# Two key stages in hand-written order on VectorE and ScalarE, layer 0 one stage later, x put away in between

## The chip, the cores and the metric

The kernel runs on one core of one Trainium2 chip. The metric is the device time of one execution in microseconds (us). Before the change it is 2494.17 us, the median of three runs (2492.08 to 2495.93).

## What is computed

The reference is a small decoder with two layers on two sequences (batch 2) of 512 tokens of width 1024, with a context of 1024 rows per sequence. All matrix products that matter here are in float32, except the first.

```python
x = x + L0_xattn(layernorm(x), ctx)      # both fake-quantized to 0..255, then x1 @ ctx
x = x + L0_ffn(layernorm(x))             # linear layer, plus a LoRA that a router weights
x = x + L1_xattn(layernorm(x), ctx)      # 32 query heads, 8 key/value heads of 128, rope on q and k
x = x + L1_ffn(layernorm(x))             # linear layer, plus the LoRA of one of 4 experts
```

The part that the change touches is the start: the product of layer 0 (the first line) and the keys and values of layer 1, which need the context alone and so can be made before x is ready:

```python
k = (ctx @ wk); k = k * cos + rotate_half(k) * sin      # 1024 x 1024 by 1024 x 1024, per sequence
v = (ctx @ wv)
q1, q2 = clip(round(x1 / s1 + z1), 0, 255), clip(round(ctx / s2 + z2), 0, 255)
layer0 = ((q1 - z1) * s1) @ ((q2 - z2) * s2)
```

## The kernel before

**Products.** Each large product is cut into two by two quarters and done with seven products instead of eight. The sums of quarters that this needs are made on VectorE: four for a weight (`left_steps`, lines 242 to 254) and four for the context (`right_steps`, lines 256 to 268). Products 1 and 2 need the raw quarters alone, so they can start before the sums. `seven` (line 270) takes the products in the order 1, 2, 6, 7, 5, 4, 3. Products 1 and 2, 7 and 4, 5 and 3 add into the same PSUM bank; there are four banks under the tag "b". So product 4 may begin only when VectorE has read 7 (line 291), and product 3 only when it has read 5 (line 293). After products 2, 5, 4 and 3 a result is complete. For keys it gets its rope (`rope_steps`, line 213: two half copies on ScalarE, lines 216 and 217, then lines 219, 222 and 223 on VectorE, in place for three of the four results) and goes to DRAM from SyncE's queue (line 476). Values go there without rope (line 500).

**Stages.** There are four stages per sequence: keys of weight half 0 and 1, values of weight half 0 and 1. Each has two groups of seven products. For sequence 0 the first two products of all four key groups are written first (lines 1015 to 1030); then the loop at line 1034 runs the rest stage by stage.

**Layer 0.** `quantized_product(b)` (line 396) is a Python generator that runs beside the stages: `weave` (line 335) calls it once after every second product. One sequence takes 14 calls: four that load and quantize two blocks of 128 context rows each (lines 194, 197 and 198 on VectorE), four that take the layernorm of 128 rows of x (lines 163 to 176), quantize them and sum each row (lines 420 to 422), where the third and fourth also transpose the block two behind (`turned`), one that transposes the third block, one for the last and the column sums, and four products of bfloat16 numbers. Calls go on through both sequences. x is loaded at the head of the generator and stays in SBUF until layer 0's linear layer, which comes after the keys and values.

**Buffers.** Tiles come from tags with a fixed number of buffers: u8 (14 of 8 KB per partition: context quarters and their sums, x, quantized rows), u4 (17 of 4 KB: weight quarters and their sums, context rows, layernorm results), u2 (10), small (16).

**Order.** Every instruction is written for one engine[...]. TensorE's order is the written one (line 976). VectorE's is the written one only within lines 1015 to 1030 for the instructions written there; others that are ready may come between. All else, the DMA queues of SyncE and ScalarE too, is ordered by a planner, which works through the program with estimated times and takes what is ready, the earlier written first.

The lines in question, as they stand before:

```python
    w[1][:] = quad_sums(wk_raw[1])
    side = chain(quantized_product(0), quantized_product(1))
    ...
            if b == 0 and i < 2:
                main = chain(*first[i])
    ...
            weave(main, side, 2, 8 if b == 0 and i == 0 else 0)
```

Of the kernel before, what the change touches and what calls it, by code (L numbers as in the profile page):

```python
# [14 lines left out]
AF = mybir.ActivationFunctionType  # L15
ALU = mybir.AluOpType
# [23 lines left out]
def decoder_kernel(  # L40
# [339 lines left out]
    q_d = [[spill([P, S], f"q{b}_{hd}") for hd in range(NH)] for b in range(B)]  # L380
    wo_d = [{i: spill([P, 2, HALF], f"wo{g}_{i}") for i in (4, 5, 6, 7)} for g in range(NKV)]


    def context_quarter(b, ch, kh, queue):
        t = u8([P, 4, HALF])
# [10 lines left out]
    def quantized_product(b):  # L396
        x[b] = halves()
        for t in range(NT):
            nc.sync.dma_start(rows(b, t), x_in[b, ts(t, P), :])
        q2 = [u8([P, 4, D], BF16) for _ in range(2)]  # L400
        for k in range(NKT):
            c_t = u4([P, D])
            nc.sync.dma_start(c_t, ctx_in[b, ts(k, P), :])
            quantized(q2[k // 4][:, k % 4, :], c_t, "x2")
            if k % 2:
                yield
        x1T = u8([P, NC, S], BF16)
        rsum, l1s = [], []

        def turned(t):  # L410
            tr = ps_wide().bitcast(BF16)[:, 0 : NC * P].rearrange("p (c n) -> p c n", c=NC)
            for c in range(NC):
                nc.tensor.transpose(tr[:, c, :], l1s[t][:, ts(c, P)], ident_b)
            copy_out(x1T[:, :, ts(t, P)], tr)

        for t in range(NT):
            h = layernorm(rows(b, t))
            l1 = u2([P, D], BF16)
            quantized(l1, h, "x1")
            r = small([P, 1])  # L420
            nc.scalar.activation(h, l1, AF.Copy, accum_out=r)
            nc.vector.tensor_scalar(r, r, c_x2, None, ALU.mult)
            rsum.append(r)
            l1s.append(l1)
            if t > 1:
                turned(t - 2)
            yield
        turned(NT - 2)
        yield
        turned(NT - 1)  # L430


        cs = ps_wide()
        for n in range(2):
            for k in range(NKT):
                nc.tensor.matmul(
                    cs[:, ts(n, HALF)],
                    ones_b,
                    q2[k // 4][:, k % 4, ts(n, HALF)],
                    start=(k == 0),  # L440
                    stop=(k == NKT - 1),
                )
        csum = u4([P, D])
        nc.vector.tensor_scalar(csum, cs, kc2, c_x1, ALU.add, ALU.mult)
        yield
        for t in range(NT):
            acc = ps_wide()
# [12 lines left out]
            nc.vector.scalar_tensor_tensor(xs, y, s12, xs, ALU.mult, ALU.add)  # L460
            yield
# [374 lines left out]
    def attention(extra):  # L836

        total = B * NH
        heads, outs, kv = {}, {}, {}
        stretches = iter(())

        def begin(n):
            if n >= total:
                return
            gg = n // GRP
            if gg not in kv:
                b, g = gg // NKV, gg % NKV  # L850
                kT = u4([P, S2])
                nc.sync.dma_start(kT, kT_d[b][g])
                v = u4([P, NKT, DH])
                nc.sync.dma_start(v, v_d[b][g // 2][:, :, ts(g % 2, DH)])
                kv[gg] = kT, v
                outs[gg] = u8([P, GRP, S])
            heads[n] = Head(n, kv[gg], outs[gg][:, n % GRP, :])

        begin(0)
        for n in range(-2, total + GRP + 1):  # L860
            new, mid, old = heads.get(n + 2), heads.get(n + 1), heads.get(n)
            begin(n + 3)
            if new:
                for j in range(4):
                    new.scores(j)
            yield

            if n - 1 in heads:
                heads.pop(n - 1).normalize()
            if n == GRP - 1 or n == NH:  # L870
                x[n // NH] = halves()
                for t, d in zip(x[n // NH], x_d[n // NH]):
                    nc.sync.dma_start(t, d)

            if GRP <= n <= total and n % GRP == 0:
                oT = outs.pop(n // GRP - 1)
                sums = u8([P, 3, 2, 256])
                places = iter(range(3))
                o_ops = left_sums(
                    nc.gpsimd,  # L880
                    oT[:, 0:2, 0:256],
                    oT[:, 2:4, 0:256],
                    oT[:, 0:2, 256:S],
                    oT[:, 2:4, 256:S],
                    lambda: sums[:, next(places)],
                )
# [12 lines left out]
            for _ in range(extra.pop(n, 0)):  # L899
                next(extra["products"])  # L900
                next(tree, None)
            if n == GRP:
                w_ops = {i: output_operand(0, i) for i in (1, 6, 2, 7, 5, 4, 3)}
            for steps in (tree, *extra["later"]):
                for _ in steps:
                    pass
            extra["later"].clear()
            yield

            if mid:  # L910
                mid.place_maximum()
            if old:
                old.turn_sum()
                old.attend(0)
            if mid:
                mid.exponential(0)
            if old:
                old.den = from_row(old.den)
            if new:
                new.turn_maximum()  # L920
            if mid:
                mid.exponential(1)
            if new:
                new.nmx = from_row(new.nmx)
            if old:
                old.attend(1)
            yield
# [84 lines left out]
    ctx_ops = [ctx_raw[0], ctx_raw[2]] + [None] * 5  # L1012
    w = [wk_raw[q][0:2] + [None] * 5 for q in range(2)]
    first = [keys(0, q, ctx_ops, w[q]) for q in range(2)]
    with tc.manual_schedule(engines={mybir.EngineType.DVE}):
        rights = right_steps(nc.vector, *ctx_raw, lambda: u8([P, 4, HALF]))
        lefts = left_steps(nc.vector, *wk_raw[0], lambda: u4([P, 4, 256]))
        advance(rights, 2)
# [9 lines left out]
        for _ in range(2):  # L1028
            for g in first[1]:
                next(g)  # L1030
    w[1][:] = quad_sums(wk_raw[1])

    side = chain(quantized_product(0), quantized_product(1))
    for b in range(B):
        if b == 1:
            ctx_raw = [context_quarter(1, ch, kh, nc.scalar) for ch in range(2) for kh in range(2)]
            w = quad_weights(wk, 0)
            ctx_ops = context_sums(ctx_raw)
        for i, stage in enumerate((keys, keys, values, values)):
            if b == 0 and i < 2:  # L1040
                main = chain(*first[i])
            else:
                main = pair(*stage(b, i % 2, ctx_ops, w))
            weave(main, side, 2, 8 if b == 0 and i == 0 else 0)
            if i < 3 and (b, i) != (0, 0):
                w = quad_weights((wk, wv)[(i + 1) // 2], (i + 1) % 2)
            if i == 1 and b == 1:
                for _ in side:
# [3 lines left out]
                nc.sync.dma_start(a_t, a0T.rearrange("(c p) m -> p c m", p=P))  # L1052
                nc.gpsimd.dma_start(b_t, b0.partition_broadcast(P))  # L1053
                tT = [None] * B
                hs, steps = normed(0, u8, 2)
                side = chain(steps, routed(0, hs, a_t, b_t, tT))
    for _ in side:
# [17 lines left out]
    for b in range(B):  # L1075
# [6 lines left out]
        weave(main, side, 1 + b, 3)  # L1082
        for _ in side:
            pass

    def put_away(b):
        for t, d in zip(x[b], x_d[b]):
            nc.sync.dma_start(d, t)

    put_away(0)  # L1090
    w = [quad_weights(wq, 0), quad_weights(wq, 1)]
# [59 lines left out]
            wupT[ts(ch, 4 * P), ts(nh, HALF)].rearrange("(c p) n -> p c n", p=P),  # L1151
        )

    def fetch_rows():
        x[0] = halves()
        for t, d in zip(x[0], x_d[0]):
            nc.sync.dma_start(t, d)

    def begin_map():
        hs = last["hs"]  # L1160
        last["h"][:2] = hs[0]
# [5 lines left out]
    for i in range(2):  # L1167
# [5 lines left out]
    hooks[(61, 2)] = [  # L1173
        lambda: fetch_weight(1, 0, 0),
        lambda: fetch_weight(2, 1, 0),
        fetch_rows,
        begin_map,
    ]
    hooks[(62, 1)] = [lambda: advance(last["gates"], 4)]
# [136 lines left out]
```

## Time and profile before

| What | us |
|---|---|
| Median of three runs | 2494.17 |
| The profiled execution | 2491.89 |
| Its span, first to last instruction | 2490.1 |
| TensorE busy | 2434.2 |
| VectorE busy | 1852.5 |
| GpSimd busy | 1011.8 |
| ScalarE busy | 527.9 |

The span is what the trace covers; the execution's own time lies 1.8 us above it. TensorE is busy almost throughout, so what counts are the stretches in which it waits. Keys and values of both sequences, with layer 0, take about the first 420 us of the span; in that stretch TensorE is busy 398.2 us. A float32 product of 128 x 512 is seen in the trace as two matmul records. "L291" is line 291 of the kernel; a bracket in a timeline gives the idle time of the engine just before the instruction and what ended it.

### The profile page before, as it was taken

The page shows a single profiled execution, that of the slowest core. Times are in us where ns is not written, and L with a number is a line of the kernel's source. Part 1 is how long each engine was busy: PE and PEld are TensorE (multiplying, and loading weights), DVE is VectorE, ACT ScalarE, POOL GpSimd, SP SyncE. Part 2 cuts the span into 40 slices and gives each one's busy share as a digit, 9 for nine tenths or more (in the row PEclk, how much of TensorE's full clock was granted, in tenths as well). Part 3 has the DMA queues.
Part 4 walks back from the last instruction along what each step waited for, and adds up shares of the span by engine and source line. Part 5 has one row for each costly group of instructions (what it writes and reads, how often), then busy time and mean ns, then how long its engine had stood idle before and what let it go on. Part 6 is the DMA issues. An engine that isn't in the chain of part 4 may idle for free.

```text
span 2490.1 us, 19684 instructions
## 1 busy us (share of the span) xinstructions
PE 2434.2 (98%) x6848; PEld 1214.5 (49%) x6856; DVE 1852.5 (74%) x2036; ACT 527.9 (21%) x615; POOL 1011.8 (41%) x536
## 2 busy tenths in 40 slices
PE   7999999999999998989999999999999999999999
PEld 3477458654444443434444444444444444445454
DVE  5848774345886557988888888888898888887552
ACT  1201221011222222232222222222222222222100
POOL 0000010111000001557676767676777676667421
PEclk8999999999999999999999999999999999999999
DMA  7225233012895221343323322442334233323301
GB/s 264 103 92 204 75 124 106 26 68 106 283 329 199 76 93 47 102 131 107 84 80 109 109 83 80 138 150 79 114 106 130 62 104 114 104 74 110 127 26 43
DMA packets 148243, 283.83 MB, mean 114 GB/s; under 512 B 29296, under 2 KB 47232, under 8 KB 146352
## 3 DMA queue, kind: packets, MB, share of 16 engines
q1 hardware_dynamic: 107888, 242.25, 28.7%
q10 hardware_dynamic: 39824, 39.60, 6.6%
q8 instruction: 55, 0.90, 0.2%
q0 software_dynamic: 432, 0.71, 0.1%
q14 instruction: 44, 0.36, 0.0%
HBM read 221.44 MB, written 61.08 MB: 113 GB/s over the span
## 4 chain that ended last, share of the span: by engine, by line
PE 59%; DVE 7%; POOL 2%; issue 2%; DMA 1%; ACT 1%; SPq 0%; POOLq 0%; DVEq 0%; ACTq 0%
PE b L347 26%; PE wide L748 15%; PE b L811 15%; PE wide L712 2%; DVE u L794 2%; DMA u<-in_wo_dram 1%; PE wide L937 1%; DVE u L772 1%; DVE u L774 1%; DVE small L714 1%; POOL u L804 1%; POOL u L803 0%; DVE u L762 0%; DVE u L222 0%; DVE u L219 0%
## 5 line engine op out<-in xcount | busy, mean ns | idle before, releaser
L347 PE MATMUL b<-u,u 128*128 128x512 f32 (+1 forms) x3648 | 1408.6, 543 | 25.3 <-DVE u L291 10.8
L347 PEld LDWEIGHTS b<-u,u 128*128 128x128 f32 x3648 | 691.4, 191 | 707.5 <-issue 619.4
L748 PE MATMUL wide<-u,u 128*128 128x512 f32 x1024 | 456.9, 597 | 15.7 <-DVE small L714 8.5
L811 PE MATMUL b<-u,u 128*128 128x512 f32 x1024 | 461.2, 593 | 0.0
L800 POOL TENSOR_TENSOR u<-u 128x1024 f32<-128x1024 f32 x64 | 151.6, 2369 | 747.4 <-DMA row<-small 385.0
L762 DVE TENSOR_TENSOR u<-wide,u 128x1024 f32<-128x1024 f32 x256 | 312.7, 1224 | 128.2 <-PE wide L748 127.8
L797 ACT ACTIVATE u<-u 128x2048 f32<-128x2048 f32 x128 | 244.6, 1911 | 675.7 <-DVE u L794 626.4
L748 PEld LDWEIGHTS wide<-u,u 128*128 128x128 f32 x1024 | 193.4, 191 | 268.0 <-issue 176.8
L794 DVE TENSOR_TENSOR u<-u,b 128x2048 f32<-128x2048 f32 x128 | 290.0, 2266 | 0.0
L811 PEld LDWEIGHTS b<-u,u 128*128 128x128 f32 x1024 | 186.7, 192 | 185.2 <-issue 185.2
L322 POOL TENSOR_TENSOR u<-u,u 128x512 f32<-128x512 f32 x120 | 189.4, 1599 | 195.0 <-DVE u L320 175.4
L320 DVE TENSOR_TENSOR u<-u,b 128x512 f32<-128x512 f32 x200 | 135.7, 679 | 135.1 <-PE b L347 135.1
L803 POOL TENSOR_TENSOR u<-u,u 128x1024 f32<-128x1024 f32 x64 | 150.8, 2356 | 35.6 <-ACT u L797 34.6
L804 POOL TENSOR_TENSOR u<-u,u 128x1024 f32<-128x1024 f32 x64 | 151.9, 2374 | 5.0
L822 POOL TENSOR_TENSOR u<-u,u 128x512 f32<-128x512 f32 x64 | 119.9, 1873 | 21.4 <-DMA u<-row 21.4
L1053 POOL DMA_DIRECT2D u<-in_b_dram x1 | 0.6, 558 | 301.8 <-PE wide L450 301.8
L216 ACT ACTIVATE u<-u 64x512 f32<-64x512 f32 x72 | 45.2, 628 | 344.6 <-DVE u L293 167.3
L712 PEld LDWEIGHTS wide<-ident,u 128*128 128x128 f32 x512 | 80.2, 204 | 64.6 <-issue 54.7
L770 DVE TENSOR_TENSOR u<-u 128x1024 f32<-128x1024 f32 x64 | 111.4, 1741 | 0.0
L772 DVE TENSOR_TENSOR u<-u,u 128x1024 f32<-128x1024 f32 x64 | 106.3, 1660 | 0.2
L805 POOL TENSOR_TENSOR u<-u 128x512 f32<-128x512 f32 x64 | 102.0, 1594 | 5.0
L774 DVE TENSOR_TENSOR u<-u,u 128x1024 f32<-128x1024 f32 x64 | 97.4, 1522 | 0.2
(125 smaller groups left out, 1552.3 us busy)
## 6 DMA issues: line engine op xcount, KB each, us to landing
u<-row ACTq DMA_DIRECT2D x128, 256.0 KB, 3.7
u<-wo SPq DMA_DIRECT2D x64, 512.0 KB, 4.0
u<-in_wo_dram SPq DMA_DIRECT2D x48, 512.0 KB, 4.5
u<-in_wq_dram SPq DMA_DIRECT2D x32, 512.0 KB, 4.0
q<-u SPq DMA_DIRECT2D x64, 256.0 KB, 2.1
u<-in_wo_dram SPq DMA_DIRECT2D x16, 1024.0 KB, 8.1
wo<-u SPq DMA_DIRECT2D x32, 512.0 KB, 3.7
u<-q SPq DMA_DIRECT2D x64, 256.0 KB, 4.1
```

The lines of the kernel that those rows point to most:

```text
L320: nc.vector.tensor_tensor(c, c, acc, ALU.add)
L322: nc.gpsimd.tensor_tensor(c, c, u, ALU.add)
L347: nc.tensor.matmul(acc, lhsT, rhs, start=start and k == 0, stop=k == len(pairs) - 1, skip_group_check=True,)
L748: nc.tensor.matmul(sc[:, ts(n, HALF)], self.kT[:, ts(2 * j + n, P)], self.qT, start=True, stop=True,)
L762: nc.vector.tensor_tensor(self.e[j // 2][:, js, :], sc.rearrange("p (k q) -> p k q", k=2), mask[j], ALU.add)
L772: nc.vector.tensor_tensor(m, m, e[1][:, 0:2, :], ALU.max)
L794: nc.vector.tensor_tensor(e, e, self.nmf.unsqueeze(1).to_broadcast([P, 4, S]), ALU.add)
L797: nc.scalar.activation(e, e, AF.Exp)
L800: nc.gpsimd.tensor_tensor(d, e[:, 0:2, :], e[:, 2:4, :], ALU.add)
L803: nc.gpsimd.tensor_tensor(d, d, e[:, 0:2, :], ALU.add)
L804: nc.gpsimd.tensor_tensor(d, d, e[:, 2:4, :], ALU.add)
L811: nc.tensor.matmul(self.acc, self.v[:, k, :], self.e[j][:, k % 4, :], start=(k == 0), stop=(k == NKT - 1),)
```

## The change

It has five parts.

1. The first two key stages of sequence 0, whole, stand in a block in which VectorE and ScalarE keep the written order. The four sums of the second weight half are written after results 5 to 8 of the first stage (g0's last product and g1's first three). The sums of the first value weight (`wv`) are written at the end of this block.
2. Layer 0 begins in the second key stage instead of late in the first: five calls there, none before.
3. The row sums move from the block's own call into `turned`, so they stand two blocks behind. The row sum's ScalarE pass writes its unused copy to a new u4 tile instead of over the layernorm result.
4. Once layer 0 is done for sequence 0, its x goes to DRAM (`put_away(0)`), and it is fetched again (`fetch_rows(0)`) before the layernorm of the linear layer.
5. Two of the four context quarters of sequence 1, the ones that its first two products read, are loaded before the last value stage of sequence 0; the other two stay where they were.

`put_away` and `fetch_rows` existed before and are moved up; `fetch_rows` takes the sequence as an argument now.

```diff
@@ quantized_product, turned
             copy_out(x1T[:, :, ts(t, P)], tr)
+            r = small([P, 1])
+            nc.scalar.activation(u4([P, D]), l1s[t], AF.Copy, accum_out=r)
+            nc.vector.tensor_scalar(r, r, c_x2, None, ALU.mult)
+            rsum.append(r)
...
             quantized(l1, h, "x1")
-            r = small([P, 1])
-            nc.scalar.activation(h, l1, AF.Copy, accum_out=r)
-            nc.vector.tensor_scalar(r, r, c_x2, None, ALU.mult)
-            rsum.append(r)
             l1s.append(l1)
@@
-    with tc.manual_schedule(engines={mybir.EngineType.DVE}):
+
+    def layer_0():
+        yield from quantized_product(0)
+        put_away(0)
+        yield from quantized_product(1)
+
+    side = layer_0()
+    with tc.manual_schedule(engines={mybir.EngineType.DVE, mybir.EngineType.Activation}):
         rights = right_steps(nc.vector, *ctx_raw, lambda: u8([P, 4, HALF]))
...
         for _ in range(2):
             for g in first[1]:
                 next(g)
-    w[1][:] = quad_sums(wk_raw[1])
-
-    side = chain(quantized_product(0), quantized_product(1))
+        lefts = left_steps(nc.vector, *wk_raw[1], lambda: u4([P, 4, 256]))
+        for i, _ in enumerate(chain(*first[0])):
+            if i in (4, 5, 6, 7):
+                w[1][:] = next(lefts) or w[1]
+        weave(chain(*first[1]), side, 2)
+        w = quad_weights(wv, 0)
+
     for b in range(B):
         if b == 1:
-            ctx_raw = [context_quarter(1, ch, kh, nc.scalar) for ch in range(2) for kh in range(2)]
+            for ch in range(2):
+                ctx_raw[2 * ch + 1] = context_quarter(1, ch, 1, nc.scalar)
             w = quad_weights(wk, 0)
             ctx_ops = context_sums(ctx_raw)
         for i, stage in enumerate((keys, keys, values, values)):
             if b == 0 and i < 2:
-                main = chain(*first[i])
-            else:
-                main = pair(*stage(b, i % 2, ctx_ops, w))
-            weave(main, side, 2, 8 if b == 0 and i == 0 else 0)
-            if i < 3 and (b, i) != (0, 0):
+                continue
+            if (b, i) == (0, 3):
+                ctx_raw = [None] * 4
+                for ch in range(2):
+                    ctx_raw[2 * ch] = context_quarter(1, ch, 0, nc.scalar)
+            weave(pair(*stage(b, i % 2, ctx_ops, w)), side, 2)
+            if i < 3:
                 w = quad_weights((wk, wv)[(i + 1) // 2], (i + 1) % 2)
             if i == 1 and b == 1:
...
                 tT = [None] * B
+                fetch_rows(0)
                 hs, steps = normed(0, u8, 2)
```

More of the change, by code (lines that the diff above doesn't have):

```diff
@@ L381, in decoder_kernel, with put_away, fetch_rows @@
     wo_d = [{i: spill([P, 2, HALF], f"wo{g}_{i}") for i in (4, 5, 6, 7)} for g in range(NKV)]
+    def put_away(b):
+        for t, d in zip(x[b], x_d[b]):
+            nc.sync.dma_start(d, t)
+    def fetch_rows(b):
+        x[b] = halves()
+        for t, d in zip(x[b], x_d[b]):
+            nc.sync.dma_start(t, d)
     def context_quarter(b, ch, kh, queue):
@@ L870, in attention @@
             if n == GRP - 1 or n == NH:
-                x[n // NH] = halves()
-                for t, d in zip(x[n // NH], x_d[n // NH]):
-                    nc.sync.dma_start(t, d)
+                fetch_rows(n // NH)
             if GRP <= n <= total and n % GRP == 0:
@@ L1084, in decoder_kernel @@
             pass
-    def put_away(b):
-        for t, d in zip(x[b], x_d[b]):
-            nc.sync.dma_start(d, t)
     put_away(0)
@@ L1152, in fetch_weight @@
         )
[L1154 to L1157, printed above, removed]
     def begin_map():
@@ L1175, in decoder_kernel @@
         lambda: fetch_weight(2, 1, 0),
-        fetch_rows,
+        lambda: fetch_rows(0),
         begin_map,
```

## The prediction

> **What bounds the kernel now.** Part 1 of the page first: TensorE is busy nearly throughout, so an edit counts only by the gaps it opens or closes there. Then, for the first 420 us (all that the change touches), what TensorE waited for:
>
> ```profile
> PE 2434.2 (98%) x6848; PEld 1214.5 (49%) x6856; DVE 1852.5 (74%) x2036; ACT 527.9 (21%) x615; POOL 1011.8 (41%) x536
> ...
> PE b L347 <- DMA u<-in_ctxT_in_dram: 9.7, 4, 3.9
> PE b L347 <- DVE u L291: 9.6, 3, 5.9
> PE b L347 <- DMA u<-in_wk_dram: 2.1, 1, 2.1
> ```
>
> The first wait is the start-up loads, untouched. TensorE's timeline places the others (the bracket is the gap before), and the windows (window and length, busy time of TensorE, weight loads, VectorE, ScalarE and GpSimd, then granted clock, DMA share, GB/s) show what the largest left behind:
>
> ```profile
> 57.69 62.66 PE L347 MATMUL b<-u,u 128*128 128x512 f32 x144 [5.93 <-DVE u L291]
> ...
> 211.72 24.48 PE L347 MATMUL b<-u,u 128*128 128x256 f32 x112 [1.37 <-DVE u L291]
> 238.31 3.67 PE L347 MATMUL b<-u,u 128*128 128x512 f32 x8 [2.11 <-DMA u<-in_wk_dram]
> ...
> 349.30 11.07 PE L347 MATMUL b<-u,u 128*128 128x512 f32 x27 [2.26 <-DVE u L291]
> ```
> ```profile
> 52.00:56.00 4.00, 0.00 (x0) 0.00 (x0) 3.24 (x6) 1.33 (x2) 0.00 (x0) 0.94 0.99 340
> 56.00:60.00 4.00, 2.31 (x3) 1.17 (x4) 3.68 (x7) 0.25 (x1) 0.00 (x0) 0.50 1.02 411
> 60.00:64.00 4.00, 4.00 (x8) 1.60 (x7) 4.00 (x7) 1.26 (x2) 0.00 (x0) 0.71 0.82 296
> 64.00:68.00 4.00, 4.00 (x11) 1.85 (x10) 4.00 (x8) 1.26 (x2) 0.00 (x0) 1.00 0.33 127
> ```
>
> After the 5.93 us gap the clock was 0.50, then 0.71: 2.31 x 0.5 + 4 x 0.29 = 2.3 us more. So this gap costs 8.2, the four together 14 (2.26 costs about 1.3 more in clock: 0.63 over 348 to 352). That is the most that can be won.
>
> VectorE's timeline gives the prices, and SyncE's the order of loads:
>
> ```profile
> 94.62 0.69 DVE L293 TENSOR_TENSOR u<-u,b 128x512 f32<-128x512 f32 x1 [2.74 <-PE b L347]
> 96.69 0.69 DVE L219 SCALAR_TENSOR_TENSOR u<-u,u 128x512 f32<-128x512 f32 x1 [1.38 <-ACT u L217]
> 97.30 0.68 DVE L222 TENSOR_TENSOR u<-u,u 128x512 f32<-128x512 f32 x1
> 98.02 0.69 DVE L223 TENSOR_TENSOR u<-u,u 128x512 f32<-128x512 f32 x1
> 98.63 0.68 DVE L297 TENSOR_TENSOR u<-u,b 128x512 f32<-128x512 f32 x1
> ...
> 135.19 0.81 DVE L194 TENSOR_SCALAR u<-u,qp_inv_x,qp_x_zp 128x1024 f32<-128x1024 f32 x1
> 136.04 0.69 DVE L197 TENSOR_SCALAR u<-u 128x1024 f32<-128x1024 f32 x1
> 136.77 0.69 DVE L198 TENSOR_SCALAR u<-u 128x1024 bf16<-128x1024 f32 x1
> 137.38 1.28 DVE L163 BATCH_NORM_STATS2 small<-u 128x6 f32<-128x512 f32 x2
> ```
> ```profile
> 41.47 1.86 SPq L399 DMA_DIRECT2D u<-in_x_in_dram  x4
> ...
> 65.36 40.98 SPq L476 DMA_DIRECT2D kT<-u  x9
> 106.44 1.82 SPq L362 DMA_DIRECT2D u<-in_wv_dram  x4
> ```
>
> See the 1.38 us in which VectorE stands still between a drain (L293) and its rope (L219), which must let ScalarE read the tile first; and that loads with nothing to wait for stand late. x was issued at 41.47 though SyncE was free from 22.2 and more than half of the u8 buffers unused; the last rights tile, written ahead of it, is made at 42.12. I read from this that the planner hands out the buffers of a tag in written order, so a load issues only after the tiles written ahead of it exist.
>
> [...] 2.11 left it at 1.00, 2.26 did not. [...] around 334 us L219 took 2.83 instead of 0.69 beside GpSimd's L593. [...]
>
> **The change, part by part.** A product is 3.43 us (ScalarE's bank copies at 31.20 and 34.63). I call the groups g0, g1 (stage one), h0, h1 (stage two), a, b (values). Up to 44.3 us nothing differs.
>
> *Removed.* Ahead of g0's L291 stood, out of order, four weight sums (4.6) and 4.2 us of layer 0, one wait in it. Gone, L291 ends at 49.4 and g0's fourth product starts at 51.8: 5.93 and 2.3 are saved there.
>
> *What VectorE then owes in strict order.* A roped product 98.63 - 94.62 = 4.0, 1.4 of it idle; a plain one 0.6; a group of five 2 x 0.6 + 3 x 4.0 = 13.2, against 17.2 of TensorE. Weight sums 4.7 (L245 to L253 at 187.75 to 192.43). A side step of two context rows 2 x (137.38 - 135.19) = 4.4; that with the first layernorm 5.1 and a 1.3 table load. From g0's L293 at 51.9: g0 12.0, sums 4.7, g1 13.2, h0 13.2, four side steps 17.5, h1 to its fourth product's rope 9.2: 69.8, so 122 us. In the old order other work filled the idle 1.4s; now what is written next waits. TensorE goes short in stage two: h0's fourth product wants L291 at 86.1 and gets it at 87.8; h1's wants it at 105.0, and it stands behind side step three, at 109.8; h1's fifth waits for L293 to 114.9. Stage two ends at 118.3, against 118.5 now (transposes at 121.91, less a product): the 8.2 saved are spent again, in smaller pieces.
>
> *Next late: wv.* Its loads take u4 buffers written after the first layernorm's h (L168), the last but one VectorE work of the block. So on SyncE they fall behind h1's fourth kT store, which waits for the rope at 122. Now they come at 106.44, 12 us before need. From 122.2 and 3.84 (wk: issued 234.47, TensorE on at 238.31) values start at 126.1: 7.8 of standing after 118.3, plus 2.3 of clock as after 5.93, +10.1. The bounds: nothing, if the loads pass that store (issue at 114 or sooner)[...]. I take 10.1. The wv sums (s2 at 134.4) and the second layernorm (139.7) are then covered by the late start (a's third product at 140); without it they cost 2 each.
>
> *Row sums.* Eight ScalarE passes of 1.06 us and eight L422 of 0.2, same count, after the transposes instead of before. In place before, now a u4 tile each. ScalarE is 21% busy; layernorm's next statistics (109.56) no longer queue behind L421. Zero on TensorE, plus or minus 0.5.
>
> *Side one call later.* 33 calls instead of 34, 29 needed: the transposes and products of layer 0 move by one slot, no more work.
>
> *x away and back.* Two 1 MB stores after L460, two 1 MB loads back, all on SyncE; x of the second half is loaded after layer 0's first half instead of at 120.7, so 2 MB of stores and 2 MB of x meet its 4 MB of context rows (landing 9.1 us per MB beside others). Behind the stores on SyncE stand those rows, behind them VectorE's L194, behind it the drains: the 1.37 at 211 can go or grow to 4. I take -0.5.
>
> *Context sooner.* Two of four 1 MB loads leave ScalarE's queue at about 135 instead of 200 and more. wk's loads follow the first instead of the second layernorm of that half, some 10 us sooner: the 2.11 goes. Hidden if anything else holds SyncE: 0.
>
> *At 347.* x's statistics, made at 264 to 269 now, go behind the fetch, at most 6 us into a full stretch (VectorE 19.93 of 20 in 320 to 340); one half of x finds free buffers early. The 2.26 + 1.3 may vanish or double: -1.
>
> Sum: -8.2 + 8.0 (the stalls within stage two) + 10.1 - 0.5 - 2.1 - 1 = +6.3 on the profiled execution's 2491.9 (span 2490.1 and 1.8 around it); the median shown, 2494.2, is 2.3 above it: 2500.5.
>
> **Rivals.** *Even (0.27).* The same shortage on VectorE, but wv's loads pass the store or VectorE's chain is 4 us shorter (ropes 3.8, rows 3.9): values start 0 to 4 late, the later gaps give 3.6: 2491 to 2495. For it: row steps take 3.9 where mixed. Against: the kT stores and loads keep written order in the trace. *Faster (0.18).* One mechanism: shorter waits or work slipped into them keep VectorE in step through stage two, so that neither L291 is late. TensorE would then end stage two at 51.8 + 17 x 3.43 = 110.1, wv would come 4.4 after that (h1's fourth product ends at 106.7, rope 4.0, load 3.8), so values start 4.0 sooner than now; with 2.1, 0.5 and 1 later on, 7.6: 2486.6. It passes 0.2% below from a chain of about 61 us in place of my 69.8. For it: VectorE was only 72 and 80% busy in 80 to 100 and 100 to 120. Against: in strict order its waits are part of the chain. *Much slower (0.05).* The fetched x or the crowded loads stop TensorE once more for over 5 us: 2508 and above. *No effect*: excluded, the order of VectorE changes from 44 us on.
>
> **How the numbers follow.** 0.2% of this kernel is 5 us, about what a measurement can tell from no change: 2489.2 to 2499.2 is "same". Likeliest case 0.50, its own range 2496 to 2507, six sevenths of it slower. Slower 0.43 + 0.05 + 0.02; faster 0.17 + 0.05 (the even case with all later gaps gone); same the rest, 0.28. The range 2485 to 2508 leaves out a third of the faster case, the last case and a little of the tails.
>
> **What would show it.** Right: no gap at 52; TensorE gaps on L291 around 86 and 105; a gap on wv near 118 to 126, wv issued behind a kT store at about 122; none on wk. Wrong: wv issued before 114, or VectorE idle before h1's drains.

## The result, and the profile after

The changed kernel takes 2498.05 us (median of 19 runs, 2494.64 to 2501.26); the kernel before, run beside it, 2493.29 (19 runs). The ratio is 1.0016, interval [1.0010, 1.0023]: some 4 us slower, a difference larger than its uncertainty but inside the 0.2% that the prediction called "same" (only the upper end of the interval lies above it). The forecast was 2500.5.

The profiled execution of the changed kernel happens to be its fastest run, 2494.64 us with a span of 2492.9. Some line numbers of the changed kernel have moved: the loads of x are now line 408, those of the context rows 412, the bfloat16 transposes 422, the kT stores 485, the v stores 509. First what TensorE did, and what it waited for in the first 420 us (total, times, longest):

```profile
PE 2435.7 (98%) x6848; PEld 1215.9 (49%) x6856; DVE 1851.1 (74%) x2036; ACT 528.0 (21%) x615; POOL 1010.9 (41%) x536
...
PE b L347 <- DVE u L291: 7.9, 3, 4.9
PE b L347 <- DMA u<-in_ctxT_in_dram: 7.4, 3, 4.0
PE b L347 <- DMA u<-in_wv_dram: 7.4, 1, 7.4
PE b L347 <- ACT u L284: 1.6, 1, 1.6
```

The wait on wk is gone and one on wv, of more than three times its size, has come. TensorE's timeline of the changed kernel says where (start, duration, instruction; the gap before it in the bracket):

```profile
86.61 17.43 PE L347 MATMUL b<-u,u 128*128 128x512 f32 x40 [1.68 <-DVE u L291]
108.92 9.24 PE L347 MATMUL b<-u,u 128*128 128x512 f32 x16 [4.87 <-DVE u L291]
125.55 12.94 PE L347 MATMUL b<-u,u 128*128 128x256 f32 x48 [7.39 <-DMA u<-in_wv_dram]
140.52 7.17 PE L347 MATMUL b<-u,u 128*128 128x256 f32 x32 [1.59 <-ACT u L284]
...
355.68 17.49 PE L347 MATMUL b<-u,u 128*128 128x512 f32 x64 [1.35 <-DVE u L291]
```

The 5.93 us gap of stage one, the 1.37 at 211 and the 2.11 at 238 are no longer there. In their place stand 1.68 and 4.87 within stage two, 7.39 ahead of the values and 1.59 a few products later. The windows (as in the prediction: length, busy time of TensorE, weight loads, VectorE, ScalarE, GpSimd, then clock, DMA share, GB/s) show that the two larger gaps left a slow clock behind:

```profile
108.00:112.00 4.00, 3.08 (x4) 1.51 (x5) 3.81 (x7) 0.00 (x0) 0.00 (x0) 0.50 0.01 4
112.00:116.00 4.00, 4.00 (x9) 1.63 (x8) 2.57 (x5) 1.25 (x2) 0.00 (x0) 0.85 0.00 0
...
124.00:128.00 4.00, 2.45 (x6) 1.99 (x7) 3.62 (x9) 0.63 (x3) 0.00 (x0) 0.50 1.00 399
```

VectorE's timeline shows why h1's L291 is late. Side step three (two context rows, quantized, from 103.04 on) stands ahead of it, to the end, and the products run out meanwhile, at 104.04:

```profile
105.22 0.81 DVE L194 TENSOR_SCALAR u<-u,qp_inv_x,qp_x_zp 128x1024 f32<-128x1024 f32 x1
106.06 0.69 DVE L197 TENSOR_SCALAR u<-u 128x1024 f32<-128x1024 f32 x1
106.79 0.69 DVE L198 TENSOR_SCALAR u<-u 128x1024 bf16<-128x1024 f32 x1
107.40 0.68 DVE L288 TENSOR_TENSOR u<-u,b 128x512 f32<-128x512 f32 x1
108.17 0.69 DVE L291 TENSOR_TENSOR u<-u,b 128x512 f32<-128x512 f32 x1
```

And SyncE's queue shows the five kT stores up to that of h1's fourth product, and the loads of wv behind them:

```profile
90.78 30.81 SPq L485 DMA_DIRECT2D kT<-u  x5
121.64 1.87 SPq L362 DMA_DIRECT2D u<-in_wv_dram  x4
```

**Where the time went.** A mark late in the stretch that differs is the first transpose of x's layernorm (line 204, float32): 368.19 before, 373.01 after, 4.8 later. That this is about the 4.76 between the medians is partly chance: the two profiled spans differ by 2.8 alone, since the rest after the mark is 2.0 shorter. Up to the first value product the kernel loses 125.55 - 118.48 = 7.1 (118.48 is the transposes at 121.91, less a product of 3.43); from there to the mark it wins 2.3 back. One caution on such differences: in the profiles of all kernels of this study the long second stretch of products begins between 12.0 and 14.7 us (the start-up loads), and the rest after the mark takes 2119.6 to 2125.7, with no pattern that I can tie to an edit. One profile against another is good to some 3 us; the ratios, from 5 to 22 runs each, decide.

### The profile page after: what moved, and what is told of

It is laid out like the page before. It is cut to its first block, busy times and chain, and to the rows that moved or that the text cites. A ratio compares the mean times of both kernels' runs of the same rounds, so it can differ in the third digit from the quotient of the medians.

```text
span 2492.9 us, 19686 instructions
## 1 busy us (share of the span) xinstructions
PE 2435.7 (98%) x6848; PEld 1215.9 (49%) x6856; DVE 1851.1 (74%) x2036; ACT 528.0 (21%) x615; POOL 1010.9 (41%) x536
## 4 chain that ended last, share of the span: by engine, by line
PE 59%; DVE 7%; issue 2%; DMA 1%; POOL 1%; ACT 1%; SPq 0%; POOLq 0%; ACTq 0%; DVEq 0%
PE b L347 26%; PE wide L757 16%; PE b L820 15%; PE wide L721 2%; DVE u L803 2%; DMA u<-in_wo_dram 1%; DVE u L781 1%; PE wide L944 1%; DVE u L783 1%; DVE small L723 1%; DVE u L771 1%; DVE u L222 0%; DVE u L219 0%; DVE u L320 0%; POOL u L813 0%
## 5 line engine op out<-in xcount | busy, mean ns | idle before, releaser
L812 POOL TENSOR_TENSOR u<-u,u 128x1024 f32<-128x1024 f32 x64 | 150.7, 2354 | 35.2 <-ACT u L806 35.0
L813 POOL TENSOR_TENSOR u<-u,u 128x1024 f32<-128x1024 f32 x64 | 151.8, 2371 | 5.0
L602 POOL TENSOR_TENSOR u<-u,u 128x1024 f32<-128x1024 f32 x8 | 20.2, 2528 | 231.3 <-DVE u L168 228.7
```

Of the source, the lines that this page charges most:

```text
L812: nc.gpsimd.tensor_tensor(d, d, e[:, 0:2, :], ALU.add)
L813: nc.gpsimd.tensor_tensor(d, d, e[:, 2:4, :], ALU.add)
```

## The experiments

Two questions: what sets the start of the values (the late wv, or VectorE's written order), and which of the five parts brings what. All twelve, beside the kernel before in their own session:

| Kernel | Ratio to before | Interval | First L204 at, us |
|---|---|---|---|
| changed kernel | 1.0016 | 1.0010 to 1.0023 | 373.01 |
| 1 wv sooner | 1.0034 | 1.0023 to 1.0046 | 375.98 |
| 2 stage two left to the planner | 0.9974 | 0.9965 to 0.9983 | 364.24 |
| 3 parts 3 to 5, old beginning | 0.9991 | 0.9983 to 0.9999 | 363.83 |
| 4 parts 1 and 2 alone | 1.0072 | 1.0058 to 1.0087 | 388.94 |
| 5 ropes one product behind | 0.9965 | 0.9953 to 0.9978 | 361.89 |
| 6a without part 3 | 1.0012 | 1.0005 to 1.0019 | 372.52 |
| 6b parts 1 to 3 | 1.0047 | 1.0035 to 1.0060 | 383.20 |
| 7 as 2, x behind the context rows | 0.9997 | 0.9990 to 1.0004 | 370.02 |
| 8 as 5, wv sooner, layernorm later | 0.9995 | 0.9987 to 1.0003 | 369.48 |
| 9 without part 4 | 1.0055 | 1.0043 to 1.0068 | 380.99 |
| 10 as 7, first sequence alone | 0.9958 | 0.9944 to 0.9972 | 362.18 |
| 11 without part 5 | 1.0017 | 1.0011 to 1.0024 | 376.46 |

### 1. The loads of wv ahead of stage two

```diff
+        raw = quad_loads(wv, 0)        # the four loads of quad_weights, without its sums
         weave(chain(*first[1]), side, 2)
-        w = quad_weights(wv, 0)
+        w = quad_sums(raw)
```

> As the changed kernel, but the four loads of the first wv half are written ahead of stage two instead of behind it; the sums stay behind it. Theory A (the wait on wv comes from the written order of the u4 buffers, which puts the loads behind a kT store on SyncE): wv is issued by about 75 us, the gap of 7.4 before the first values product and its 2.2 us of clock go, VectorE's backlog then costs about 2 at the wv sums and 1.5 at the second layernorm: 6 us faster than the changed kernel, about 1 below the kernel before. Rival B (TensorE waits for VectorE's chain in any case, the load only happens to be named): the gap moves to the sums, at most 2 us faster than the changed kernel.

2500.82 us, ratio 1.0034: the wait on wv is gone and nothing is won. TensorE's timeline of this kernel, one line of what VectorE waited for between 40 and 140 us (total, times, longest), and then ScalarE's timeline:

```profile
88.89 20.14 PE L347 MATMUL b<-u,u 128*128 128x512 f32 x40 [4.97 <-DVE u L291]
111.21 15.74 PE L347 MATMUL b<-u,u 128*128 128x512 f32 x48 [2.18 <-DVE u L291]
134.06 6.01 PE L347 MATMUL b<-u,u 128*128 128x256 f32 x16 [7.12 <-ACT u L284]
```
```profile
DVE u L194 <- DMA u<-in_ctx_in_dram: 3.1, 2, 1.8
```
```profile
132.13 0.63 ACT L216 ACTIVATE u<-u 64x512 f32<-64x512 f32 x1 [3.54 <-DVE u L300]
132.77 0.63 ACT L217 ACTIVATE u<-u 64x512 f32<-64x512 f32 x1
133.42 0.58 ACT L284 COPY u<-b 128x512 f32<-128x512 f32 x1
```

L284 copies the first value product out of PSUM. On ScalarE, in written order too, it stands behind the two rope copies of stage two's last result, and those wait for VectorE's L300, late behind layer 0's rows and layernorm. Part of this lateness the edit makes itself: the context rows, now loaded after wv, come later, and VectorE stands 3.1 us for them. So h0's gap is 4.97 instead of 1.68, h1's 2.18 instead of 4.87, and L300 starts at 131.36 instead of 129.07. ScalarE's timeline of the changed kernel, where the rows come in time, settles more:

```profile
129.84 0.63 ACT L216 ACTIVATE u<-u 64x512 f32<-64x512 f32 x1 [3.54 <-DVE u L300]
130.48 0.63 ACT L217 ACTIVATE u<-u 64x512 f32<-64x512 f32 x1
131.13 0.29 ACT L175 ACTIVATE small<-small,eps_t 128x1 f32<-128x1 f32 x1
131.62 0.59 ACT L284 COPY u<-b 128x512 f32<-128x512 f32 x1 [0.19 <-PE b L347]
```

There, too, ScalarE is busy until 131.4 with what had to wait for L300 or stands behind it, and L284 waits only 0.19 for its product. The third value product adds into the bank that L284 reads. With wv at hand when stage two ends at 118.16, two products would have run to about 125 and the third would have stood until about 132; it began at about 135 (125.55 and 12.94, less its own 3.5). So, by an estimate from this trace, wv in time is worth some 3 us at most as long as VectorE is late, and not the 7.39 and the slow clock behind it. The wait on wv was for the larger part a cover: take it away, and the lateness of VectorE comes through ScalarE. The theory that wv's place in the queue alone costs the time fell. No run moved wv with the rows left ahead of it and VectorE as late.

### 2. Stage two left to the planner

The hand-written block ends before stage two; all parts are kept otherwise.

```diff
-        weave(chain(*first[1]), side, 2)
-        w = quad_weights(wv, 0)
+    weave(chain(*first[1]), side, 2)
+    w = quad_weights(wv, 0)
```

> As the changed kernel, but the hand-written block ends before stage two, so the planner orders VectorE and ScalarE there; layer 0 still starts in stage two. Theory A (strict order leaves 1.4 us of VectorE idle at each of the ropes, 12 of them, and that alone makes it late): other work fills the idle time in stage two, no L291 is late there, values start at 110 to 114 instead of 125.5: about 10 us faster than the changed kernel, 5 or more faster than the kernel before. Rival C (it is the amount of work, layer 0 pressed into one stage, not the order): L291 is late by as much as in the changed kernel, no more than 2 us faster.

2487.02 us, ratio 0.9974: some 10 us below the changed kernel, for two lines moved out of the block. VectorE stands for L217 6 times, 8.2 us, between 40 and 126 us, where the changed kernel has 11 times, 15.1. No TensorE gap remains in stage two, and the next of any size is 2.63 on L284 at 129.83. A new one stands in stage one, on g0's L291, which the block had kept in time. TensorE's timeline of this kernel there, and VectorE's:

```profile
56.21 70.54 PE L347 MATMUL b<-u,u 128*128 128x512 f32 x184 [4.39 <-DVE u L291]
```
```profile
45.27 1.29 DVE L163 BATCH_NORM_STATS2 small<-u 128x6 f32<-128x512 f32 x2 [0.92 <-DMA u<-in_x_in_dram]
...
49.57 0.16 DVE L176 RECIPROCAL small<-small 128x1 f32<-128x1 f32 x1 [1.10 <-ACT small L175]
...
55.49 0.67 DVE L291 TENSOR_TENSOR u<-u,b 128x512 f32<-128x512 f32 x1
```

Layer 0's first layernorm, no longer in the block, is free to go where x is ready, and x is ready at 45. It goes in front of L291, with a wait for x's load and one for ScalarE, whose table load (1.28 us in this trace) stands before the first square root. TensorE waits 4.39.

### 3 and 4. The two halves of the change apart

Three keeps the old beginning (hand-written order for the first two products only, layer 0 from late in stage one) and adds parts 3 to 5. Four has the new beginning, parts 1 and 2, and nothing else.

```diff
 # 3: instead of the block's new lines
+    weave(chain(*first[0]), side, 2, 8)
+    weave(chain(*first[1]), side, 2)
+    w = quad_weights(wv, 0)
 # 4: no put_away(0), no fetch_rows(0), row sums and the four context loads where they were
```

> The beginning as in the kernel before (block on VectorE alone, layer 0 from the end of stage one, sums of the second weight left to the planner); row sums two behind, x away and back, and the two context quarters sooner as in the changed kernel. Theory A: the gap of 5.9 before stage one's fourth product is back, the later gaps at 211 and 236 are gone and that at 347 is smaller: 3 to 4 us faster than the kernel before. Rival D (the later parts cost as much in loads as they win): within 1 us of the kernel before.

> The written order of both stages and the later start of layer 0 alone; row sums, x and context as in the kernel before. Theory A: values start 7 to 8 us late as in the changed kernel and the later gaps (1.4, 2.1, 2.3) stay: 8 to 10 us slower than the kernel before, 4 slower than the changed kernel. Rival D: same as the changed kernel within 1 us.

Three is 0.9991 of before, about 2 us faster where 3 to 4 were expected: the wait on wk is gone, but the gap at 211, which should have gone too, is still 1.19. Four is 1.0072, 18 us slower where 8 to 10 were expected. Its beginning is that of the changed kernel (1.68, 4.87 and 7.46), so the surprise comes later: gaps of 2.12 at 245.86, 3.42 at 278.48 and 5.54 at 368.93, none of which the changed kernel has in that size, while those that should have stayed, 1.37 at 211 and 2.11 on wk, are not there. Parts 3 to 5 are worth some 14 us with the new beginning and 2 with the old.

### 5. Ropes one product behind

A result's drain, and then the rope of the result before it, within the block. `keys` hands over a rope that has made its ScalarE copies but not yet its VectorE steps; `settle` finishes it one product later.

```diff
-                rope(dst, src, j, 1.0)
-                nc.sync.dma_start(kT_d[b][4 * q + 2 * i + m][:, ts(j, HALF)], dst)
+                steps = finish(i, j, dst, src)     # rope_steps, then the store
+                next(steps)                        # lines 216 and 217 on ScalarE
...
+                later.append(steps)                # lines 219, 222 and 223: after the next drain
```

> The changed kernel, but in the hand-written block each rope is finished one product later: a result's drain on VectorE, then the rope of the result before it, so VectorE no longer stands 1.3 to 1.4 us between a drain and its own rope. Nothing is left out. Theory C (the idle 1.4s inside the hand-written order are what makes VectorE late, some 11 of them between the first L293 and the end of stage two): its chain is about 15 us shorter, both TensorE gaps on L291 in stage two (1.68 and 4.87) go, the first value product starts at 112 to 116 instead of 125.55, and the kernel is 9 to 12 us faster than after: about 2487. Rival D (it is the amount of work, or the loads of wv behind the last store of the stage, that hold the values back): at most 3 us faster, 2495 or above.

2487.99 us, ratio 0.9965, some 12 us below the changed kernel. In the changed kernel the trace puts the waits that this edit takes out in one line (who waited for ScalarE's second rope copy, line 217, between 40 and 126 us: total and times):

```profile
DVE u L219: 15.1, 11
```

Without them TensorE's timeline reads as follows, and SyncE's queue after it:

```profile
84.59 17.43 PE L347 MATMUL b<-u,u 128*128 128x512 f32 x40 [0.80 <-DVE u L291]
...
107.24 3.70 PE L347 MATMUL b<-u,u 128*128 128x512 f32 x8 [1.26 <-DVE u L293]
114.74 12.31 PE L347 MATMUL b<-u,u 128*128 128x256 f32 x48 [3.80 <-DMA u<-in_wv_dram]
```
```profile
92.24 18.64 SPq L484 DMA_DIRECT2D kT<-u  x4
110.98 1.83 SPq L362 DMA_DIRECT2D u<-in_wv_dram  x4
121.00 2.26 SPq L484 DMA_DIRECT2D kT<-u  x2
```

VectorE does the same work in the same block. It stands 0.7 us for ScalarE where it stood 15.1, and 8.5 for TensorE where it stood 1.5: now it is the one that is ahead. The values start 10.8 us sooner, 9.7 if one allows for the start-up, and these 9.7 have two parts. Stage two ends at 110.94 instead of 118.16, which is 6.1 sooner without the start-up: that is VectorE in time. And the wait on wv is 3.80 instead of 7.39, because the edit also moves a store. The rope of h1's fourth product and its store now stand behind the layernorm; this rope ends only at 120.97, and wv's loads no longer wait for it. They stand behind the store of h1's third, whose rope ends at 110.54, 61 us after g0's L293. In the changed kernel the third's rope comes 66.6 us after that L293, and the fourth's, for which wv waited, 70.6.

So two things were late at the same place. Experiment 1 moved wv alone and won nothing; this one put VectorE in time and let wv pass the fourth store, and won 12 us. That VectorE's standing for ScalarE makes stage two late is shown, here and by experiment 2. How much of the 12 us would have come with the fourth store still ahead of wv is not: no run separates them. By an estimate it is little: with that rope at 120.97, and values 4.3 us after it as in the changed kernel, they would have started at about 125.

### 6a, 6b, 9 and 11. Which later part

6a takes part 3 out of the changed kernel (the row sums go back into the block's own call), 6b takes out parts 4 and 5, nine part 4 alone and eleven part 5 alone.

```diff
 # 9
     def layer_0():
         yield from quantized_product(0)
-        put_away(0)
         yield from quantized_product(1)
...
-                fetch_rows(0)
 # 11
-            for ch in range(2):
-                ctx_raw[2 * ch + 1] = context_quarter(1, ch, 1, nc.scalar)
+            ctx_raw = [context_quarter(1, ch, kh, nc.scalar) for ch in range(2) for kh in range(2)]
```

> The changed kernel without its third part (the row sums go back into the block's own call). If the later parts 4 and 5 carry the 13 us that separate the changed kernel from its beginning alone: 2497 to 2500. If part 3 does, because a row sum in the block's own call stands on ScalarE in hand-written order and waits there for VectorE: 2505 or above.

> The new beginning (parts 1 and 2) with part 3, but without x put away and fetched (part 4) and without the earlier context (part 5). If parts 4 and 5 carry the 13 us: about 2510, with the wait of 2.1 on L293 near 246, of 3.4 on L291 near 278 and of 5.5 near 369 still there. If part 3 does: 2498 to 2503.

> The changed kernel without its fourth part: x of the first sequence stays in SBUF instead of going to DRAM and back. With part 5 (the context sooner) kept. If part 5 is what the later 10 to 13 us hang on: 2497 to 2500, no wait on L293 near 246. If part 4 is, through the six or so buffers that it frees before the second context and the second sequence's rows: 2506 to 2509, as with parts 1 to 3 alone.

> The changed kernel without its fifth part (all four context loads of the second sequence where they stood before), parts 1 to 4 kept. Without part 4 the fifth part was worth nothing (2508.6 against 2507.9). If part 4's free buffers do it all: 2497 to 2500, no wait near 246. If both are needed, part 5 because it spreads the 4 MB that otherwise meet x, the rows and wk on the way in: 2502 to 2506, with a wait of 2 or more on L293 near 246 or on wk.

With part 4 the kernels lie at 1.0012 (4 and 5), 1.0016 (3, 4 and 5) and 1.0017 (3 and 4); without it at 1.0047 (3), 1.0055 (3 and 5) and 1.0072 (none). Part 4, x put away, is worth about 10 us beside parts 3 and 5 and 7 to 8 beside part 3 alone; part 5 nothing that can be measured, with part 4 or without; part 3 nothing once 4 and 5 are there. Without them it is worth perhaps 6 us (the two intervals just touch): the gap at 278 is gone in 6b, where I had expected to find it still. TensorE's timeline of the ninth kernel, and one stretch of its VectorE's:

```profile
244.03 14.02 PE L347 MATMUL b<-u,u 128*128 128x256 f32 x40 [2.06 <-DVE u L293]
361.96 19.20 PE L347 MATMUL b<-u,u 128*128 128x512 f32 x64 [5.62 <-DVE u L291]
```
```profile
343.67 2.81 DVE L219 SCALAR_TENSOR_TENSOR u<-u,u 128x512 f32<-128x512 f32 x1
346.41 2.83 DVE L222 TENSOR_TENSOR u<-u,u 128x512 f32<-128x512 f32 x1
```

At 244 VectorE stood 3.09 us for a context quarter: two loads that the changed kernel issues within 2.9 us from 217.51 on are issued at 216.57 and 231.65 here. Ahead of 362 it stood 3.53 us for wv and then ran four steps of its ropes at 2.8 us instead of 0.7, each beside an addition on GpSimd (line 602, 2.9 us each). In the changed kernel only two of them meet the ropes ahead of that L291, and the wait for wv is 0.51. That x's buffers are what holds the context load back is my reading; no run gave the loads other buffers.

### 7, 8 and 10. Towards a faster version

Seven is the second kernel with x loaded behind the context rows, for both sequences; ten the same for the first sequence only.

```diff
     def quantized_product(b):
-        x[b] = halves()
-        for t in range(NT):
-            nc.sync.dma_start(rows(b, t), x_in[b, ts(t, P), :])
         q2 = [u8([P, 4, D], BF16) for _ in range(2)]
...
+        x[b] = halves()                       # 10: here for b == 0, above for b == 1
+        for t in range(NT):
+            nc.sync.dma_start(rows(b, t), x_in[b, ts(t, P), :])
         x1T = u8([P, NC, S], BF16)
```

Eight is the fifth kernel with the loads of wv written right after the last context rows, and the first layernorm written after the block instead of in it:

```diff
+        raw = []
+
+        def four_then_loads():
+            for _ in range(4):
+                next(side)
+                yield
+            raw.extend(quad_loads(wv, 0))
-        weave(behind(chain(*first[1])), side, 2)
+        weave(behind(chain(*first[1])), four_then_loads(), 2)
         settle()
-        w = quad_weights(wv, 0)
+        w = quad_sums(raw)
```

> The second experiment (the hand-written block ends before stage two) with the loads of x written behind those of the first context rows, so that layer 0's first layernorm cannot come into stage one. Nothing is left out. If that layernorm ahead of L291 is what cost 4.39 us and some 2 us of clock there: the gap at 56 goes, 5 to 6 us faster than the second experiment's 2487.0: about 2481. If the rows or the first weight sums of wv then stand in the same place instead: 2486 to 2488.

> The fifth experiment (ropes finished one product behind) with two things moved: the loads of wv are written right after the last context rows, ahead of the stores of the stage, and layer 0's first layernorm is written after the block instead of in it. Nothing is left out. Now that VectorE is in time, the late wv should be the only thing that keeps the values waiting: the gap of 3.80 on wv and the 1.59 on ScalarE's copy go, values start at 110 to 111, 4 to 5 us faster than the fifth experiment: 2483. If VectorE or ScalarE still sets the start (as in the first experiment, where taking the wv wait away only uncovered a wait on L284): 2487 to 2489.

> The seventh experiment (block ends before stage two, x loads behind the context rows), but for the first sequence alone; in the second, x is loaded first, as in the changed kernel. Nothing is left out. The seventh run lost 7.42 and 1.8 us of slower clock at 251 on ScalarE's copy L284, behind the second sequence's late layernorm. If the late x load of that sequence is the reason, this stretch is full again: about 9 us faster than 2495.5, that is 2486. If not, 2494 or more.

Seven does what it should at the beginning (stages one and two run from 13.0 to 108.3 without a gap) and loses it all at 251, a wait of 7.42 on ScalarE's L284: with x late in the second sequence too, that copy of a key product stood on ScalarE behind two square roots of x's layernorm, the first of which had waited 9.30 us for VectorE, and behind a copy of transposes and a row sum. Eight has no wait on wv or L284 at the values any more (TensorE runs from 117.52 to 138.49 without a gap), and 5.31 on L291 in stage one instead: the layernorm, written after the block, ran at 45.55, inside stage one, as in the second kernel. Both missed their numbers. In eight a piece that is written later in the program did not run later; in seven it did, and the late layernorm of the second sequence then stood ahead of a copy for which TensorE waited. Ten, with x late for the first sequence only, came out as expected and has the lowest time of all: 2485.25 us, ratio 0.9958. Its interval overlaps those of five and two, so which of the three is fastest stays open. TensorE's timeline of it, with stages one and two in one unbroken stretch:

```profile
14.18 96.72 PE L347 MATMUL b<-u,u 128*128 128x512 f32 x218 [1.24 <-DMA u<-in_ctxT_in_dram]
115.15 12.31 PE L347 MATMUL b<-u,u 128*128 128x256 f32 x48 [4.25 <-DMA u<-in_wv_dram]
```

What is left there is the 4.25 on wv, with 1.7 us of slow clock behind it, and the 1.59 on L284 a few products later. A version with that taken away as well was not run.

## Why the prediction was right or wrong

**The sum and the time.** Predicted were +6.3 and 2500.5 us; measured +4 (the ratio) to +4.8 (the medians), 2498.05. The direction is that of the likeliest case and the time lies in its own range of 2496 to 2507, but by the 0.2% bound the result is "same", to which I gave 0.28, not "slower", which had 0.50. The forecast was too slow by 2.4 us: 0.9 of it is the base (2494.17, three runs, against 2493.29, 19 runs), 1.5 is the sum. Step by step, with 1.25 us taken off the predicted times of what TensorE sets, since its long stretch of products begins that much sooner in this profile (13.44 against 14.69):

**The gap removed in stage one: right.** L291 of g0 ends at 49.66 (49.4 predicted; VectorE comes to this point at the same time as before, with L267 at 42.13 and 42.12, so nothing is taken off), and stage one has no gap. The "14" that the prediction calls the most that can be won left out the 1.3 of clock that it names itself; its own figures give 15.2.

**VectorE in strict order: right, nearly to the step.** L291 of h0 ends at 86.56 (86.55) and of h1 at 108.86 (108.55); gaps of 1.68 and 4.87 where the working gives 1.7 and 4.8. The third stall, the wait for L293, did not appear, and a slow clock that I had not counted did: h1's last two products (eight records each) took 9.24 us instead of 6.86, 2.4 more. At full clock the first of them would have ended at 112.35, and L293, which ends at 113.82, would have kept TensorE 1.5; the slower TensorE gave VectorE that time. Stage two ends at 118.16 (117.05): the term of 8.0 was 1.1 too small.

**wv: right on what the trace shows, wrong on what it means.** Issued at 121.64 behind that store, gap 7.39 for 7.8, and the first 48 records of the values 12.94 us instead of the 10.6 at full clock, 2.3 for 2.3. But the step said that the late loads cost 10.1 and the bounds began at "nothing, if the loads pass that store". The first experiment let them pass, and the kernel became no faster: the copy L284 on ScalarE was late as well, and by the estimate given there wv in time was worth some 3 us at most. The prediction named who is queued behind VectorE for SyncE and left ScalarE out, which part 1 also puts in written order. Nor has it the 1.59 us ahead of 140.52, which are of another kind. There L284 stands on ScalarE behind the copy of layer 0's first transposed block (line 156), and that waits for TensorE:

```profile
138.97 1.01 ACT L156 COPY u<-wide 128x1024 bf16<-128x1024 bf16 x1 [5.72 <-PE wide L422]
139.88 0.59 ACT L284 COPY u<-b 128x512 f32<-128x512 f32 x1
```

The same 1.59 stands in experiments 5 and 10, where VectorE is in time, and not in 6a, without part 3.

**Row sums: right in the sum.** Without part 3 the ratio is 1.0012 against 1.0016. But the nothing is made of two things: in 6a the 1.59 is gone and 1.25 on L291 at 270.38 has come. And without parts 4 and 5 part 3 does count, as said.

**The later gaps: the term was mis-sized, and the credit misplaced.** Predicted -0.5, -2.1 and -1, together -3.6. Measured: 1.37 and 2.11 gone, the last gap 0.9 smaller and without its slow clock (17.49 instead of 19.06 for the 64 records), 6.0 in all, less the new 1.59: 4.4 net. This is 0.8 more than I had; against it the values start 0.7 later than predicted (125.55, for 124.85). So the working gives 6.3, and the trace, corrected for the start-up, 373.01 - 368.19 + 1.25 = 6.1. That these agree so closely is luck, since the terms were off by 1.1 one way and by 0.4 and 0.8 the other. What lies between them and the measured 4 to 4.8 is in no step: start-up and the rest after the mark differ from profile to profile by as much. But "x away and back" at -0.5 and "context sooner" at -2.1 had the wrong order: part 5 is worth nothing, even the wait on wk stays away without it (experiment 11, with two gaps of 1.6 and 1.3 near 258 and 274 instead), and part 4 is worth 8 to 10 us, because the new beginning without it opens gaps that I did not look for (experiment 9). In experiment 4, without parts 3 to 5, neither the 1.37 nor the 2.11 is there, and in experiment 3, with them and the old beginning, the gap at 211 is: what removed the 1.37 was the new beginning. I had priced parts 3 to 5 against the gaps of the kernel before; they were to be priced against the gaps of a kernel with parts 1 and 2, in which layer 0 is later and meets other work.

**The rivals.** "Faster" was put at 2486.6 should VectorE keep in step, with the point where it decides at "a chain of about 61 us in place of my 69.8". The change itself did not do it: its chain is 70.6. The fifth experiment came to 2487.99 with a chain of 61, but that is the chain to the third product's rope, behind whose store wv stood there, so that the two figures meet is luck. The way is the one named there, waits with "work slipped into them": what I thought of as another way in which the change could go was the way to mend it, and the fence with the 1.38 us in which VectorE stands still already showed where. "Even", 2491 to 2495, fell with both of its conditions: wv did not pass the store, and the chain was not 4 us shorter. Of "much slower" nothing came: no later gap exceeds 1.6 us.

## What to carry to other kernels

In the strict order of this block VectorE's waits were time that its later work paid: with 0.7 us of standing for ScalarE in place of 15.1, stage two ended 6.1 us sooner (experiment 5). Before writing such an order out, add up the handoffs to another engine (here 11 of 1.4 us) and put other work between the two halves of each. A wait that stands last ahead of a gap can be a cover: ask what else is late at that moment before pricing its removal, and move the two together. And price a part of a change against the kernel that the other parts leave, not against the one that stands now: the same three parts were worth 2 us and 14.

## What was not expected of the hardware

The slow clock cost less here than it took. After the 4.87 us gap TensorE lost 2.4 us to it, yet in the same stretch a wait of about 1.5 us (the estimate above) went away. After the same gap the loss differs from profile to profile: six kernels have a gap of 4.86 or 4.87 there, and the 16 records behind it take 8.83 (experiment 11) to 9.45 us (experiment 4), 2.0 to 2.6 more than the 6.86 at full clock. Over gaps of different length the loss was 3.0 us after 4.09 (experiment 7), 1.7 after 3.80, 4.25 and 5.62 (experiments 5, 10 and 9), 2.4 after 4.87 and 2.3 after 7.39 (the changed kernel), and 1.7 after 7.42 (experiment 7), so in these runs it does not grow with the gap. What it goes with shows when the windows are laid on the edges of the slow clock, twice in the changed kernel and once in the fifth:

```profile
106.40:113.20 6.80, 4.29 (x5) 1.85 (x6) 6.54 (x11) 0.00 (x0) 0.00 (x0) 0.50 0.01 2
123.40:130.30 6.90, 4.75 (x11) 3.81 (x12) 5.48 (x12) 1.70 (x4) 0.00 (x0) 0.51 0.73 292
```
```profile
115.90:119.30 3.40, 3.40 (x9) 2.70 (x8) 3.40 (x8) 0.16 (x1) 0.00 (x0) 0.50 0.80 311
```

The clock is at half here for 3.4 or some 6.8 us, and what is lost is about half of the part of it in which TensorE works: of 4.29, 4.75 and 3.40 us that is 2.1, 2.4 and 1.7. Gaps of nearly the same length differ in whether they leave a slow clock at all. In the kernel before, 2.11 us left the clock at 1.00 over 240 to 244, and 2.26 were followed by 0.63 over 348 to 352. One of 2.18 in the first experiment left 1.8 us of slow clock behind (an estimate from the 15.74 us of the 48 records after it), while one of 2.27 in the third left none (17.49 us for the 64 records, as in the changed kernel).
